# Convolution stage of a two-layer Fourier kernel: reciprocals and angle rounding in smaller pieces, second-half moments and v's statistics at later steps

## The chip, the cores and the metric

The kernel runs on one core of one Trainium2 chip. The metric is the device time of one execution in microseconds (us). Before the change it is 2817.53 us, the median of three runs that lie between 2812.63 and 2821.07. The profiled execution spans 2806.7 us, at a mean granted TensorE clock of 0.976 of full speed.

Engine names are those of the profile: PE is TensorE's matmul, PEld its weight load, DVE is VectorE, ACT is ScalarE, POOL is GpSimd, SP is SyncE, whose queue (SPq) issues nearly all transfers of this stage.

## The reference

The input x has shape 16 x 16 x 256 x 256 (images, channels, rows, columns), float32. Two layers follow each other:

```python
x = x + _L0_conv_ref(_gn(x), L0_conv_weight)      # a circular 3x3 convolution, written with FFTs
x = x + _L1_conv_ref(_gn(x), ty, tx, poles1, poles2, residues)   # a Laplace neural operator

def _gn(v, G=8, eps=1e-5):       # group norm: 8 groups of 2 channels, per image
    g = v.reshape(B_, G, C_ // G, H_, W_)
    m = jnp.mean(g, axis=(2, 3, 4), keepdims=True)
    s = jnp.var(g, axis=(2, 3, 4), keepdims=True)
    return ((g - m) / jnp.sqrt(s + eps)).reshape(v.shape)
```

Layer 1 needs tables made of the poles: reciprocals `1 / (omega - pole)` for all frequencies, and exponentials `exp(pole * t)`, whose imaginary part asks for sines of large angles, rounded to within pi first. These tables depend on the small weights alone, not on x.

## The kernel before

The kernel has four stages, one after the other: the convolution (about 29 to 642 us), the spectra (to about 1290 us), the mixing of channels (to about 1990 us), and the way back to the output. The change lies wholly in the first.

**The loop of the convolution stage.** `for g in range(24 * B + 3)` walks 387 steps, 24 for each of 16 images. Below, n is the step within an image, g modulo 24. At each step `conv(g)` (L225) issues 16 small matmuls (32 x 32 weights against 32 x 512 data, two records of line L239 each in the trace) that run side by side on four row groups and four column groups of the array. Every third step two PSUM tiles are full, and ACT evicts them as `vt` (L256), adds the bias and, by accumulators, their sums and squares. DVE then makes first moments of v from a quarter of the tiles (`bn_stats`, L258), and two steps later the mirrored sum and difference of lower and upper rows (`mirror`, L221 and L222, 128 x 1024 each). SP stores both to `vD` a step after that (L282).

**What else is put between the steps.** All engines execute their own instructions in the order in which the Python program emits them, so the loop's body is a schedule written by hand. At each step, in this order: `conv(g)`; one piece of `early`; loads of x; pieces of `x_stats` that are due; pieces of the two chains of tables.

- *Loads of x*: image b+2's first half at n = 3 and second half at n = 15 (L113, 2322 KB each, five buffers `xt`).
- *`x_stats(b)`* (L149) computes the group norm of image b, and with it the scaled weights `wc` and the bias, before step 24b. It yields pairs of a due time (steps before 24b) and a piece: 16 `moments` (`bn_stats`, L156), eight for each half of the image; `bn_aggr` (L164); a small matmul over the channels (`spread`, L168); `about_mean` (L176 to L178); a second `spread`; `root` (L184 on DVE, then a square root on ACT, L185); `conv_weights` (L144 to L201); a third `spread`; `biases` (L207, L208). The three matmuls stand in PE's order among those of the convolution, so PE stops at each until DVE has delivered its operand. They share one PSUM buffer, `ps_stat`. The bias column lies in the tile `xq`, of which there are two in turn.
- *Two chains of tables* of layer 1. One advances a piece every second step: `make_poles`, `make_hat` (twice two halves, with a reciprocal of 128 x 512, L420), `make_c` (eight rounds, with a reciprocal of 128 x 512, L566). The other advances a piece every fifth step: `make_exps` (twice eight rounds, with three `scalar_tensor_tensor` and two `tensor_scalar` for the rounding of the angles, L496 to L498), `make_coef`.
- *`early`*, a generator of `v_stats` (L291), turns the sums of the first 12 images of v into the scale and mean of layer 1's group norm. It has six pieces: many small DVE operations, a matmul (L312), more of them (L314 to L324), a matmul (L332), a square root, and a last refinement with two reciprocals of 128 x 192. Its two matmuls write `ps_stat` too. It advances when `g > 24 * (B - 4) + 8 and g % 3 == 0`, so at steps 9, 12, 15, 18, 21 and 24 after g = 288.

Of the kernel before, what the change touches and what calls it, by code (L numbers as in the profile page):

```python
# [16 lines left out]
B = 16  # L17
# [7 lines left out]
def conv_then_laplace_kernel(ctx: ExitStack, tc: tile.TileContext, a: dict, out: bass.AP):  # L25
# [15 lines left out]
    nc = tc.nc  # L41
# [83 lines left out]
    g128 = load1("g128", [P, P], tp)  # L125
# [23 lines left out]
    def x_stats(b):  # L149


        st = sp.tile([P, C, 6], FP, name="xst", tag="xst")

        def moments(j):
            r0 = 1 + 2 * (j % 8)
            nc.vector.bn_stats(st[:, j, :], halves[b][j // 8][:, r0 : r0 + 2, 1 : N + 1])  # L156

        for j in range(8):
            yield 38 - j, lambda: moments(j)
        for j in range(8, C):  # L160
            yield 33 - j // 2, lambda: moments(j)
        q = sp.tile([P, 12], FP, name="xq", tag="xq")
        mean, pvar, mu, d, e, var, sd, tmp, r, nb, bias = (q[:, j : j + 1] for j in range(11))
        yield 24, lambda: nc.vector.bn_aggr(q[:, 0:2], st)  # L164

        def spread(lhs, rhs):
            ps = pst.tile([P, 512], FP, name="ps_stat", tag="ps_stat")
            nc.tensor.matmul(ps[:, 0:1], lhsT=lhs, rhs=rhs, start=True, stop=True)  # L168
            return ps[:, 0:1]

        ps = []
        yield 18, lambda: ps.append(spread(g128, mean))

        def about_mean():

            nc.vector.tensor_copy(mu, ps[0])  # L176
            nc.vector.tensor_tensor(d, mean, mu, ALU.subtract)
            nc.vector.scalar_tensor_tensor(e, d, d, pvar, ALU.mult, ALU.add)  # L178

        yield 17, about_mean  # L180
        yield 14, lambda: ps.append(spread(g128, e))

        def root():
            nc.vector.tensor_scalar(var, ps[1], 1e-5, None, ALU.add)  # L184
            nc.scalar.activation(sd, var, AF.Sqrt)  # L185

        yield 12, root
        wc = sp.tile([P, 2, 3, 32], FP, name="wc", tag="wc")

        def conv_weights():  # L190
            newton(sd, var, tmp)
            nc.vector.reciprocal(r, sd)
            nc.vector.scalar_tensor_tensor(
                wc.rearrange("p h t m -> p (h t m)"),
                wband.rearrange("p h t m -> p (h t m)"),
                r,
                imask.rearrange("p h t m -> p (h t m)"),
                ALU.mult,
                ALU.add,
            )  # L200
            nc.vector.tensor_scalar(nb, mu, r, -1.0, ALU.mult, ALU.mult)  # L201

        yield 9, conv_weights
        yield 5, lambda: ps.append(spread(wsum.rearrange("p c m -> p (c m)"), nb))

        def biases():
            nc.vector.tensor_copy(bias, ps[2])  # L207
            nc.vector.tensor_scalar(shift[:, b : b + 1], mu, -1.0, None, ALU.mult)  # L208
            ready[b] = wc, bias

        yield 3, biases
# [171 lines left out]
    def make_hat(side):  # L383

        hatT = wp.tile([P, 6 * N], FP, name="hatT", tag="hatT")
        hatT = hatT[:, 0 : 2 * N].rearrange("p (j e t) -> p j e t", j=2, e=2)  # L390
        nc.sync.dma_start(out=hatT, in_=a[f"hatT{side}"])
        om = sw.tile([P, 3], FP, name="s_kcol", tag="s_kcol")
        nc.sync.dma_start(out=om[:, 0:1], in_=a["kcol"])
        om1, om2, scale = (om[:, j : j + 1] for j in range(3))
        to = ((tabE[:, 1:], tabO[:, :C]), (hB[:, 0], hB[:, 1]))[side]
        n = C * C * 2
        for half in range(2):
            tags = "s_re0", "s_re1", "s_pb", "s_im0", "s_im1", "s_den0", "s_den1"
            tiles = [
                sw.tile([P, 2 * n if t == "s_pb" else n], FP, name=t, tag=t)[:, 0:n] for t in tags  # L400
            ]
            pr, npi, m, sq, nb, g, b2 = tiles
            at = slice(half * n, half * n + n)
            for j in range(5):
                nc.sync.dma_start(out=tiles[j], in_=hD[j, side, at].partition_broadcast(P))
            yield
            yield
            if half == 0:
                omega(om1, om1, rd[:, side : side + 1])
                nc.vector.tensor_tensor(om2, om1, om1, ALU.mult)  # L410
                nc.vector.tensor_scalar(scale, cols[:, 17:18], -1.0, 1.0, ALU.mult, ALU.add)
                nc.vector.tensor_tensor(scale, scale, om1, ALU.add)
                nc.vector.tensor_scalar(hatT[:, 1], hatT[:, 1], scale, None, ALU.mult)
            yield
            nc.scalar.activation(g, sq, AF.Square, bias=om2)
            nc.scalar.activation(b2, nb, AF.Square)
            yield
            nc.gpsimd.tensor_tensor(g, g, b2, ALU.add)
            yield
            nc.vector.reciprocal(g, g)  # L420
            yield
            for z in (pr, npi, nb):
                nc.gpsimd.tensor_tensor(z, z, g, ALU.mult)
            yield
            nc.vector.scalar_tensor_tensor(sq, sq, om2, g, ALU.add, ALU.mult)
            yield
            nc.vector.scalar_tensor_tensor(pr, m, om2, pr, ALU.add, ALU.mult)
            nc.vector.scalar_tensor_tensor(npi, m, om2, npi, ALU.subtract, ALU.mult)
            for j, z in ((5, sq), (6, nb)):
                nc.sync.dma_start(out=z[0:1], in_=hD[j, side, at].unsqueeze(0))  # L430
            yield
            yield
            for eo in range(2):
                hv = to[eo].rearrange("p i (m r) -> p i m r", r=2)[:, 8 * half : 8 * half + 8]
                for ri, parts in enumerate(((pr, sq), (npi, nb))):
                    ps = psu.tile([P, 512], FP, name="ps_setup", tag="ps_setup")
                    for j, src in enumerate(parts):
                        nc.tensor.matmul(
                            ps, lhsT=hatT[:, j, eo], rhs=src, start=j == 0, stop=j == 1
                        )  # L440
                    yield
                    nc.scalar.copy(hv[:, :, :, ri], ps.rearrange("p (i m) -> p i m", i=8))
                    yield
# [24 lines left out]
    def make_exps(which):  # L468
# [10 lines left out]
        for q in range(8):  # L479
# [13 lines left out]
            c2 = float(np.float32(1.93500518798828125e-3))  # L493
            c3 = 2 * np.pi - c1 - c2
            for c in (c1, c2, c3):
                nc.vector.scalar_tensor_tensor(th, rn, -float(c), th, ALU.mult, ALU.add)  # L496
            nc.vector.tensor_scalar(th, th, phase, 3.1415925, ALU.add, ALU.min)
            nc.vector.tensor_scalar(th, th, -3.1415925, None, ALU.max)  # L498
            yield
# [14 lines left out]
    def make_c():  # L514
# [8 lines left out]
        z = space[:, 2 * N : 2 * N + 64].rearrange("p (j k) -> p j k", j=4)  # L523
# [30 lines left out]
        for k0 in range(0, C, 2):  # L554

            at = k0 // 2 % 2
            den = sw.tile([P, 2, N], FP, name="s_cden", tag=f"s_den{at}")
# [5 lines left out]
                nc.gpsimd.tensor_scalar(den[:, j], den[:, j], pr2[:, k : k + 1], None, ALU.add)  # L563
                nc.gpsimd.tensor_scalar(num[:, j], om, nm1, s0[:, k : k + 1], ALU.mult, ALU.add)
            yield
            nc.vector.reciprocal(den, den)  # L566
            w = sw.tile([P, 2, 4, 2, 4, 8], FP, name="s_w", tag=f"s_im{at}")
            for odd in range(2):
                for st in range(2):
# [10 lines left out]
                        ALU.mult,  # L580
                    )
            yield
            yield
            nc.gpsimd.tensor_tensor(num, num, den, ALU.mult)
            yield
# [2 lines left out]
            for i0 in range(0, 4, 2):  # L588
                c = c4[:, i0 : i0 + 2]
                ps = psu.tile([P, 2, N], FP, name="ps_setup", tag="ps_setup")  # L590
# [22 lines left out]
    def chain(*gens):  # L613
        for gen in gens:
            yield from gen
# [8 lines left out]
    for b in range(1, B):  # L624
        at_step.setdefault(max(0, 24 * b - 40), []).append((b, x_stats(b)))
    going = []
    tables = (
        (2, 0, chain(make_poles(), make_hat(0), make_hat(1), make_c())),
        (5, 1, chain(make_exps(0), make_exps(1), make_coef())),
    )  # L630
    early = v_stats(0, B - 4, lambda: pst.tile([P, 512], FP, name="ps_stat", tag="ps_stat"))
    for g in range(24 * B + 3):
        conv(g)
        if g > 24 * (B - 4) + 8 and g % 3 == 0:
            next(early, None)
        b, n = divmod(g, 24)
        if b + 2 < B and n == 3:
            halves[b + 2] = [load_x(b + 2, 0)]
        if b + 2 < B and n == 15:
            halves[b + 2].append(load_x(b + 2, 1))  # L640
        for b, gen in at_step.get(g, ()):
            going.append([b, gen, next(gen)])
        for it in list(going):
            while it[2] is not None and g >= 24 * it[0] - it[2][0]:
                it[2][1]()
                it[2] = next(it[1], None)
            if it[2] is None:
                going.remove(it)
        for every, first, gen in tables:
            if g % every == first:  # L650
                next(gen, None)
# [30 lines left out]
    m, n = cols[:, 16:17], cols[:, 17:18]  # L682
# [773 lines left out]
```

## Time and profile before

| | busy, us | share of the span |
|---|---|---|
| PE | 2616.8 | 93% |
| DVE | 1928.3 | 69% |
| ACT | 1522.8 | 54% |
| POOL | 1075.6 | 38% |

These shares cover the whole execution. The convolution stage is read by itself: the trace gives the busy time of every engine in any stretch, and the starts of the convolution's matmuls, 32 records to a step, tell when each step began. From these starts the 16 images took, in us: 35.4, 46.3, 38.3, 36.3, 50.6, 41.2, 34.2, 37.5, 34.5, 36.9, 36.7, 36.8, 50.4, 40.2, 28.9 and 28.3 (the last with the loop's end). The page's list of costliest groups gives for each line its busy time, the mean of one instruction, and how long the engine was idle just before it and for whom. The list of waits sums those idle times by waiting line and releaser. A window's timeline lists the instructions in order of time.

### The profile page before, as it was taken

Reading aid. Unit: us, or ns where it says so; the run is one execution under the profiler, and the core shown is the slowest. Engines: PE = TensorE matmul, PEld = TensorE weight load, DVE = VectorE, ACT = ScalarE, POOL = GpSimd, SP = SyncE. Lnnn points to the kernel's source line nnn. Section 1 sums busy time; section 2 is a strip of 40 time slices with the busy share of each in tenths; the row PEclk is TensorE's granted clock in tenths of the full one; section 3 lists DMA queues with packets and bytes.
Section 4 is the critical chain, followed back from the end, with each engine's and each line's share of the span. In section 5 each row is a group of like instructions: output and inputs, shape, how many; then the busy total and the mean of one; then the engine's idle time right before and its main releaser. Section 6 shows DMA issues by size and latency. Waiting matters only on the chain.

```text
span 2806.7 us, 93073 instructions
## 1 busy us (share of the span) xinstructions
PE 2616.8 (93%) x39600; PEld 1958.4 (70%) x39600; DVE 1928.3 (69%) x3562; ACT 1522.8 (54%) x3090; POOL 1075.6 (38%) x997
## 2 busy tenths in 40 slices
PE   5878988797999999996999999999989999999998
PEld 2434444355777777774888888888778888888887
DVE  6888998867888888885454444444346666666666
ACT  3767777664666666663455555555434444444443
POOL 1543466513333333334111111111165656565653
PEclk9999999898999999998999999999999999999999
DMA  7776887655665656654766666676688999989995
GB/s 270 255 248 247 286 285 267 230 185 166 229 229 208 213 203 240 227 193 162 200 189 194 190 192 192 194 195 193 198 274 284 289 284 288 283 286 286 288 284 179
DMA packets 479375, 652.82 MB, mean 233 GB/s; under 512 B 51352, under 2 KB 457880, under 8 KB 465008
## 3 DMA queue, kind: packets, MB, share of 16 engines
q1 hardware_dynamic: 477248, 637.56, 70.5%
q8 instruction: 312, 5.11, 0.7%
q0 software_dynamic: 1568, 5.11, 0.6%
q10 hardware_dynamic: 144, 4.19, 0.3%
q14 instruction: 103, 0.84, 0.1%
HBM read 367.22 MB, written 279.50 MB: 230 GB/s over the span
## 4 chain that ended last, share of the span: by engine, by line
PE 61%; DVE 14%; DMA 12%; POOL 4%; issue 4%; SPq 2%; ACT 1%; DVEq 0%; POOLq 0%; ACTq 0%
PE ps_mix L1028 16%; PE ps_s L962 9%; PE ps_y L720 8%; PE ps_y L728 8%; DMA yk<-yD 6%; PE ps_x L763 4%; PE ps_conv L239 4%; PE ps_p L1212 3%; DVE r L1245 3%; PE ps_f L1236 3%; PE ps_f L1237 3%; DMA out_y<-ol 3%; DVE xst L156 2%; DMA xt<-in_x 2%; SPq L1159 2%
## 5 line engine op out<-in xcount | busy, mean ns | idle before, releaser
L1028 PEld LDWEIGHTS ps_mix<-abd,sg 128*64 128x64 f32 x8192 | 449.1, 138 | 61.5 <-ACT sg L1085 48.9
L1028 PE MATMUL ps_mix<-abd,sg 128*64 128x128 f32 x8192 | 480.0, 276 | 9.5 <-ACT yt L1090 9.5
L239 PE MATMUL ps_conv<-xt,wc 32*32 32x512 f32 x12288 | 463.3, 618 | 27.2 <-issue 24.8
L1176 POOL TENSOR_TENSOR u<-yk 128x512 f32<-128x512 f32 (+1 forms) x268 | 346.0, 1322 | 317.7 <-PE ps_p L1212 210.3
L736 ACT ACTIVATE t<-ps_y,vmr 128x384 f32<-128x384 f32 x512 | 297.2, 581 | 166.7 <-PE ps_y L728 166.6
L239 PEld LDWEIGHTS ps_conv<-xt,wc 32*32 32x32 f32 x12288 | 231.4, 105 | 214.4 <-issue 139.4
L933 POOL TENSOR_TENSOR w<-v,mcol 128x2048 f32<-128x2048 f32 x33 | 119.3, 3616 | 575.3 <-DVE v L930 546.9
L1090 DVE COPY yt<-ps_mix 128x512 f32<-128x512 f32 x128 | 88.5, 691 | 360.7 <-PE ps_mix L1028 238.5
L720 PE MATMUL ps_y<-tabE,vq 128*128 128x256 f32 x1024 | 313.5, 388 | 15.0 <-DVE vq L709 13.4
L728 PE MATMUL ps_y<-tabO,vq 128*128 128x256 f32 x1024 | 306.1, 381 | 0.0
L1236 PE MATMUL ps_f<-pt,inv 128*128 128x256 f32 x1008 | 300.4, 380 | 0.0
L1090 ACT COPY yt<-ps_mix 128x512 f32<-128x512 f32 x384 | 220.5, 586 | 146.5 <-PE ps_mix L1028 88.4
L1237 PE MATMUL ps_f<-hs,ey 128*128 128x256 f32 x1008 | 299.8, 379 | 0.0
L1212 PEld LDWEIGHTS ps_p<-inv,u 128*128 128x128 f32 x2048 | 266.0, 193 | 45.0 <-issue 25.1
L1212 PE MATMUL ps_p<-inv,u 128*128 128x128 f32 x2048 | 279.4, 280 | 8.4 <-POOL u L1180 8.3
L962 PE MATMUL ps_s<-ct,w 64*32 64x256 f32 x8448 | 261.2, 382 | 24.4 <-POOL abd L977 24.1
L1240 DVE TENSOR_TENSOR r<-ps_f,q 128x256 f32<-128x256 f32 x256 | 106.9, 418 | 251.5 <-ACT q L1239 251.5
L1085 ACT COPY sg<-ps_s 128x512 f32<-128x512 f32 x248 | 159.7, 645 | 190.7 <-PE ps_s L962 190.6
L720 PEld LDWEIGHTS ps_y<-tabE,vq 128*128 128x128 f32 x1024 | 189.7, 191 | 91.5 <-ACT q L776 50.3
L256 ACT ACTIVATE vt<-ps_conv,xq 128x512 f32<-128x512 f32 x256 | 167.0, 680 | 155.9 <-PE ps_conv L239 140.7
L1239 ACT COPY q<-ps_f 128x256 f32<-128x256 f32 x256 | 95.4, 372 | 287.6 <-PE ps_f L1237 284.4
L1214 ACT COPY pt<-ps_p 128x512 f32<-128x512 f32 x256 | 150.1, 586 | 133.3 <-PE ps_p L1212 117.9
(238 smaller groups left out, 4170.4 us busy)
## 6 DMA issues: line engine op xcount, KB each, us to landing
xt<-in_x SPq DMA_DIRECT2D x32, 2322.0 KB, 10.8
abd<-aD SPq DMA_DIRECT2D x512, 128.0 KB, 2.9
yD<-yt SPq DMA_DIRECT2D x512, 128.0 KB, 2.6
vl<-vD SPq DMA_DIRECT2D x256, 256.0 KB, 4.1
out_y<-ol SPq DMA_DIRECT2D x128, 512.0 KB, 9.2
s<-vD SPq DMA_DIRECT2D x244, 256.0 KB, 6.7
aD<-spec SPq DMA_DIRECT2D x15, 4096.0 KB, 12.5
yk<-yD SPq DMA_DIRECT2D x60, 1024.0 KB, 8.5
```

The costliest lines, as they stand in the source:

```text
L239: nc.tensor.matmul(acc[r][32 * c : 32 * c + 32], lhsT=ready[b][0][rows, phase, tap], rhs=halves[b][u // 2][rows, q : q + 5 : 4, 2 - tap : ...
L256: nc.scalar.activation(vt[:, r % 2], acc[r], AF.Identity, bias=ready[b][1], **by_sums)
L720: nc.tensor.matmul(ps[:, 0:N], lhsT=vf[:, xo, 0, j], rhs=tabE[:, 0 : i + 2 : i + 1], start=True, stop=False, skip_group_check=True,)
L728: nc.tensor.matmul(ps[:, P : P + N], lhsT=vf[:, xo, 1, j], rhs=tabO[:, i : C + 1 : C - i], start=False, stop=True, skip_group_check=True,)
L736: nc.scalar.activation(t[:, xo, j].rearrange("p l n -> p (l n)"), ps[:, 0:384], AF.Copy, scale=vmr[:, 0, b0 + j, i : i + 1],)
L962: nc.tensor.matmul(ps[odd][32 * iq : 32 * iq + 32, ro], lhsT=w[rows, iq, kk, ro], rhs=ct[rows, iq, kk], start=True, stop=True,)
L1028: nc.tensor.matmul(ps[64 * t : 64 * t + 64, j], lhsT=sg[:, f : f + 2].rearrange("p f m -> p (f m)"), rhs=abd[jq][:, :, 2 * t + cc, 2 * jj ...
L1090: (nc.vector.tensor_copy if m == 3 else nc.scalar.copy)(o, src)
L1176: nc.gpsimd.tensor_tensor(u[:, :, j].rearrange("p b (c n) -> p c b n", c=8), in0, in1, o)
L1212: nc.tensor.matmul(ps[:, at], lhsT=u[:, n], rhs=tab, start=True, stop=True)
L1236: nc.tensor.matmul(ps[:, e], lhsT=tab, rhs=pt[:, e], start=True, stop=False)
L1237: nc.tensor.matmul(ps[:, e], lhsT=ey[:, e], rhs=hs, start=False, stop=True)
```

## The change

Long DVE operations of the tables are cut, with a step of the loop between the pieces; the two chains of tables get other phases; the second half's moments come three steps later and the pieces that follow come one or two steps later; `early` gets its own list of steps. What it is for: other work of DVE that PE waits for should not queue behind a long piece, moments should not stand at the head of DVE's queue before their half image has landed, and the matmuls of `early` should not come between a `spread` and the piece that reads it.

```diff
@@ x_stats
         for j in range(8, C):
-            yield 33 - j // 2, lambda: moments(j)
+            yield 30 - j // 2, lambda: moments(j)
...
-        yield 24, lambda: nc.vector.bn_aggr(q[:, 0:2], st)
+        yield 22, lambda: nc.vector.bn_aggr(q[:, 0:2], st)
...
-        yield 18, lambda: ps.append(spread(g128, mean))
+        yield 17, lambda: ps.append(spread(g128, mean))
...
-        yield 17, about_mean
+        yield 16, about_mean
         yield 14, lambda: ps.append(spread(g128, e))
@@ make_hat
-            nc.vector.reciprocal(g, g)
-            yield
+            for z in (g[:, 0 : n // 2], g[:, n // 2 :]):
+                nc.vector.reciprocal(z, z)
+                yield
...
             nc.vector.scalar_tensor_tensor(pr, m, om2, pr, ALU.add, ALU.mult)
+            yield
             nc.vector.scalar_tensor_tensor(npi, m, om2, npi, ALU.subtract, ALU.mult)
@@ make_exps
             for c in (c1, c2, c3):
                 nc.vector.scalar_tensor_tensor(th, rn, -float(c), th, ALU.mult, ALU.add)
+                if c == c2:
+                    yield
@@ make_c
-            nc.vector.reciprocal(den, den)
+            nc.vector.reciprocal(den[:, 0], den[:, 0])
...
             yield
+            nc.vector.reciprocal(den[:, 1], den[:, 1])
             yield
             nc.gpsimd.tensor_tensor(num, num, den, ALU.mult)
@@ the loop
-        (5, 1, chain(make_exps(0), make_exps(1), make_coef())),
+        (4, 1, chain(make_exps(0), make_exps(1), make_coef())),
...
-        if g > 24 * (B - 4) + 8 and g % 3 == 0:
+        if g - 24 * (B - 4) in (9, 14, 17, 38, 41, 44):
             next(early, None)
```

The chain of `make_exps` advances every fourth step instead of every fifth, and has five yields to a round instead of four, so a round takes 20 steps as before. A half of `make_hat` takes 20 yields instead of 18.

## Prediction

> **What bounds the kernel now.** I read the page's time slices first. The first nine of 40 slices (70 us each) are the convolution stage; PE is busy 0.5 to 0.9 there, DVE about 0.8 to 0.9. So the stage isn't bound by matmuls alone. I then asked for the busy time in stretches that begin with each image. Columns: stretch, its length, then busy us of PE, PEld, DVE, ACT, POOL (with instruction counts), granted clock, DMA share, GB/s. Images 1, 4, 8, 12, 13, 14 and 15:
>
> ```profile
> 64.90:111.20 46.30, 37.02 (x817) 17.97 (x794) 38.92 (x61) 27.16 (x62) 24.49 (x16) 0.93 0.73 238
> ...
> 185.80:236.40 50.60, 38.11 (x812) 17.61 (x784) 42.57 (x66) 27.01 (x61) 15.88 (x11) 0.90 0.61 213
> ...
> 349.30:383.80 34.50, 31.59 (x825) 16.55 (x800) 33.88 (x50) 29.42 (x68) 26.17 (x27) 0.95 0.82 283
> ...
> 494.20:544.60 50.40, 36.28 (x850) 16.16 (x823) 44.96 (x82) 29.07 (x67) 32.92 (x38) 0.83 0.59 207
> 544.60:584.80 40.20, 31.99 (x820) 15.88 (x806) 32.32 (x52) 28.51 (x69) 5.81 (x4) 0.92 0.73 245
> 584.80:613.70 28.90, 27.34 (x777) 15.84 (x780) 21.09 (x54) 20.04 (x52) 0.00 (x0) 1.00 0.49 168
> 613.70:642.00 28.30, 28.30 (x844) 20.51 (x812) 14.44 (x16) 22.95 (x59) 8.92 (x12) 1.00 0.69 227
> ```
>
> Without DVE's table work an image takes 28 to 29 us, PE's own pace. Image 8 takes 34.5 us, of which DVE is busy 33.9: there DVE is the bound and nothing is left to win but its work. Over images 1 to 13 (64.9 to 584.8 us, one stretch) DVE is busy 452.8 of 519.9 us. Its 67.1 us of idle time are all that a new order can win there, and most of them lie in images 1, 4, 5, 12 and 13.
>
> Next the waits, DVE's own in the stage (line, releaser: us in total, times, longest), then PE's:
>
> ```profile
> DVE xst L156 <- DMA xt<-in_x: 21.6, 6, 7.5
> DVE xq L164 <- ACT vt L256: 15.9, 5, 6.5
> DVE vsum L221 <- ACT vt L256: 12.0, 7, 3.3
> DVE s_cden L566 <- POOL s_cden L563: 3.6, 3, 2.1
> ```
> ```profile
> PE ps_stat L168 <- DVE xq L164: 39.7, 7, 25.1
> PE ps_stat L168 <- DVE xq L178: 12.4, 5, 6.7
> PE ps_stat L312 <- DVE xq L184: 8.8, 1, 8.8
> PE ps_stat L168 <- DVE vmr L343: 5.3, 1, 5.3
> ```
>
> The first of PE's rows has 25.1 us of the start in it. The last is the third `spread` of an image, held because `early` still reads `ps_stat` (L343). PE stops at the small matmuls until DVE gets to their operand; DVE stops at moments whose half image hasn't landed, and at `bn_aggr`, which overwrites the `xq` tile whose bias ACT still reads at the eviction of n = 2. Each stop of one makes the other late.
>
> **What the Trainium skill says.** "TensorE: Matmul & The Clock Gate", its table at the top, gives VectorE a strict first-in-first-out queue; the trace agrees: before 187.0 us DVE stands 7.5 us at a `bn_stats`, while the evictions for the `mirror` behind it end by 184.5. "VectorE: DVE Perf Modes", The TRN2 errata, says that an operation pays a fixed latency per instruction, so cutting costs something. The trace has a reciprocal of 512 columns at 3.34 us and of 192 at 1.34, so 6.25 ns a column and 0.14 us fixed. "Perfetto Trace Analysis", Identifying the Most-Contended Engine, takes occupancy as fair for VectorE; 87% here agrees.
>
> **The change part by part.**
>
> *Second half's moments, three steps later.* Their loads are issued at n = 15 and take 10.8 us (median). Of DVE's waits for x, those before second halves are 5.5 us (image 1), 7.5 (4), 4.4 (13) and 0.4 (12), 17.8 together. Now `biases` (0.2 us) and `mirror` (1.2 + 1.4) come first, about 2.8 us. Full use gives 2.5 x 3 + 0.4, about 8; at image 13 `mirror` itself isn't ready until 585.2, so 6 is the low end. I take -8, because table pieces come ahead as well. First halves (2.2 and 1.6 us) keep their waits.
>
> *`bn_aggr` two steps later.* It then stands behind the eviction that it waits for. That wait is 15.9 us, but where DVE has run ahead it would wait at the next `mirror` instead (12.0 us there already), so between 0 and -15; I take a quarter, -4. The slack from `bn_aggr` to the first `spread` shrinks from six steps to five, from `about_mean` to the second from three to two. Behind `about_mean` DVE has only a `bn_stats` and pieces ready anyway, and PE two steps (2 us) against 0.6 us of work for three small operations: nothing where DVE is the bound.
>
> *`early` at other steps.* Now the matmul of L312 is emitted before `root` at the same step, and must wait for it (8.8 us) because both use `ps_stat`; the later stop is 5.3 us. At steps 14 and 17 of an image the buffer is free. DVE works on through both: its idle time in images 12 and 13 is 5.4 + 7.9 = 13.3 us. The 12 us of DVE work of `early` stay, half of it moves to image 13, still full. Of the idle time 2.1 and 2.8 us follow directly from PE's stops (DVE then waits for evictions at L221 and L164); with the small ones I take -4, range -1 to -9.
>
> *Tables stretched.* 1 + 1 yields in each of four half hats is 8 yields, 16 steps; `make_c` ends at step 354 instead of 338, in image 14, where DVE idles 7.8 us. About one round's reciprocal leaves the bound part: -3.5.
>
> *Reciprocals in halves.* Twelve more instructions at 0.14 us: +1.7. A first half needs only the first half of `s_cden`, so half of the 3.6 us wait for POOL goes: -2. The halves and the split rounding (2 operations, then 3, 0.77 us each at most) shorten PE's stops, from 3.3 to 1.7 us a piece, but DVE works meanwhile; worth nothing by itself. The extra yield between `pr` and `npi` is alike.
>
> *Phases 2 and 4.* At odd and even steps the two chains no longer fall on one step (at 508 to 515 us they made one block of 7.3 us). Same DVE work, so nothing counted.
>
> Sum: -8 - 4 - 4 - 3.5 + 1.7 - 2 = -19.8 us. The stages behind don't change. 2817.5 - 19.8 = 2797.7, so 2798.
>
> **The rivals.**
>
> *The idle time forms anew.* DVE's wait for x becomes a wait at `mirror` or `vsum`, PE's stop at L164 is only moved; what remains is `make_c`'s tail and a little: about -4, so 2813. For it: DVE's idle time is as small as 0.6 to 4 us an image in images 6 to 11, and PE's mid-step stops ("issue", 24.8 us, PE waiting for nothing that is shown) are untouched. Against it: the five bad images have named causes that the change addresses.
>
> *Slower.* The tighter chain makes PE stop at the second `spread` in every image: +1 us for each of 15 images, +1.7 of instructions: 2834. The 12.4 us there now, with three steps of slack, speak for it; against it, PE isn't what lasts longest in images 1 to 13.
>
> *Much faster.* If one large stop feeds the next (image 4's late x, PE's 14.9 us step, image 5's 6.5 us wait), removing the first removes all; idle falls from 67 to 25 us: -42, 2776. Transfers speak against more: 0.8 of their share is busy in images 6 to 10 at about 280 GB/s.
>
> **How the numbers follow.** The forecast gets 0.53, much faster 0.15, no change 0.17, slower 0.15. Within 0.3% is 8.5 us. Faster 0.68, same 0.17, slower 0.15. The range goes from the much-faster case, 2774, to half way to the slower one, 2822: it leaves out about 0.1 on each side or less.
>
> **What would show it.** Right: images 4 and 12 drop by 5 us or more each; DVE's wait at L156 falls from 21.6 to some 13 us; PE's waits at L312 for L184 and at L168 for L343 vanish; the stage's last matmul ends near 622 us; DVE's busy time in the stage stays within 3 us. Wrong: a larger wait of PE at L168 for L178, larger waits of DVE at L221, or a first half's moments that wait longer because DVE arrives earlier.

## The result, and the profile after

The changed kernel takes 2801.27 us (median of six runs, 2795.73 to 2805.62); the kernel before, run beside it, 2816.26 us. The ratio is 0.9947, with a 95% interval of 0.9929 to 0.9965: about 15 us faster, where 19.8 were forecast. The gain lies in the convolution stage: its last matmul starts at 626.1 us instead of 641.7 in the two profiled executions.

The same stretches as before, one for each image, here of the changed kernel (stretch, length, busy us of PE, PEld, DVE, ACT, POOL, clock, DMA share, GB/s); images 1, 4, 6, 8, 12, 13, 14:

```profile
64.10:109.20 45.10, 35.95 (x816) 15.69 (x790) 36.88 (x62) 30.21 (x67) 21.33 (x17) 1.00 0.75 269
...
185.10:228.40 43.30, 34.28 (x805) 17.21 (x779) 36.90 (x60) 29.78 (x66) 16.98 (x13) 0.92 0.70 246
...
268.10:313.20 45.10, 38.55 (x808) 17.80 (x778) 32.58 (x55) 27.32 (x62) 19.69 (x15) 0.92 0.65 231
...
348.30:381.80 33.50, 31.26 (x833) 17.07 (x812) 32.98 (x55) 29.15 (x69) 25.96 (x26) 0.95 0.85 309
...
485.00:527.40 42.40, 33.98 (x834) 17.00 (x808) 38.64 (x72) 29.98 (x71) 29.86 (x29) 0.88 0.78 270
527.40:565.10 37.70, 33.43 (x837) 17.71 (x814) 36.75 (x58) 27.38 (x68) 22.21 (x28) 0.91 0.73 262
565.10:597.70 32.60, 29.06 (x806) 15.27 (x810) 25.78 (x60) 20.92 (x57) 1.27 (x1) 1.00 0.44 150
```

Images 4 and 12 lost 7.3 and 8.0 us, as forecast. But image 6 went from 34.2 to 45.1 us and image 14 from 28.9 to 32.6: something was given back. The list of waits shows where to look. DVE's own, and three rows of PE's (line, releaser: total us, times, longest):

```profile
DVE vsum L221 <- ACT vt L256: 20.0, 11, 2.9
DVE s_th L498 <- POOL s_rn L492: 15.0, 7, 4.1
DVE xq L176 <- PE ps_stat L168: 8.1, 3, 4.4
DVE xq L164 <- ACT vt L256: 7.3, 3, 4.0
```
```profile
PE ps_stat L168 <- DVE xq L164: 32.0, 6, 25.0
PE ps_stat L168 <- DVE xq L178: 23.2, 10, 6.6
PE ps_stat L168 <- DVE vs L314: 1.8, 1, 1.8
```

The wait for x, 21.6 us before, is gone altogether. PE's stops for `early` are down from 8.8 + 5.3 to 1.8. In their place stands a row that had 4.0 us before: the rounding of the angles (L498 now) waits 15.0 us for POOL, and PE's stops at the second `spread` (L178) rose from 12.4 to 23.2. The row of the rounding in the kernel before, and the stretch of images 1 to 13, before and after:

```profile
DVE s_th L496 <- POOL s_rn L490: 4.0, 2, 2.2
```
```profile
64.90:584.80 519.90, 437.69 (x10408) 212.99 (x10385) 452.77 (x713) 370.17 (x850) 259.21 (x239) 0.94 0.75 256
```
```profile
64.10:565.10 501.00, 431.80 (x10384) 213.70 (x10360) 436.33 (x719) 368.43 (x846) 255.30 (x239) 0.95 0.77 266
```

The stretch shrank from 519.9 to 501.0 us, yet DVE's idle time in it only from 67.1 to 64.7; DVE's busy time fell instead, from 452.8 to 436.3. The total is near the forecast, the composition is not. So each part was undone in the changed kernel, and two were made alone.

### The profile page after: what moved, and what is told of

It reads as the page before. It is cut to its first block, busy times and chain, and to the rows that moved or that the text cites. A ratio compares the mean times of both kernels' runs of the same rounds, so it can differ in the third digit from the quotient of the medians.

```text
span 2793.9 us, 93071 instructions
## 1 busy us (share of the span) xinstructions
PE 2610.7 (93%) x39600; PEld 1957.2 (70%) x39600; DVE 1927.0 (69%) x3574; ACT 1516.3 (54%) x3089; POOL 1076.8 (39%) x997
## 4 chain that ended last, share of the span: by engine, by line
PE 68%; DVE 10%; DMA 8%; POOL 5%; issue 4%; ACT 2%; SPq 2%; DVEq 0%; ACTq 0%; POOLq 0%
PE ps_mix L1033 16%; PE ps_s L967 9%; PE ps_y L725 8%; PE ps_y L733 8%; PE ps_p L1217 6%; PE ps_f L1241 5%; PE ps_f L1242 5%; PE ps_x L768 4%; PE ps_conv L239 4%; DMA yk<-yD 2%; DVE r L1250 2%; DMA out_y<-ol 2%; PE psd L753 1%; DVE xst L156 1%; PE ps_h L1201 1%
## 5 line engine op out<-in xcount | busy, mean ns | idle before, releaser
L725 PE MATMUL ps_y<-tabE,vq 128*128 128x256 f32 x1024 | 313.0, 387 | 14.0 <-DVE vq L714 12.4
L967 PEld LDWEIGHTS ps_s<-ct,w 64*32 64x32 f32 x8448 | 158.9, 106 | 91.6 <-POOL abd L982 25.1
## 6 DMA issues: line engine op xcount, KB each, us to landing
aD<-spec SPq DMA_DIRECT2D x15, 4096.0 KB, 12.4
```

The source lines that it names most:

```text
L725: nc.tensor.matmul(ps[:, 0:N], lhsT=vf[:, xo, 0, j], rhs=tabE[:, 0 : i + 2 : i + 1], start=True, stop=False, skip_group_check=True,)
L967: nc.tensor.matmul(ps[odd][32 * iq : 32 * iq + 32, ro], lhsT=w[rows, iq, kk, ro], rhs=ct[rows, iq, kk], start=True, stop=True,)
```

## Experiments: the parts

Ratios below are to the kernel before, run on the same chip, with 95% intervals. "Idle" is DVE's idle time over images 1 to 13 of the profiled run.

**The later moments undone** (all the rest as changed):

```diff
-            yield 30 - j // 2, lambda: moments(j)
+            yield 33 - j // 2, lambda: moments(j)
```

> The changed kernel, with the second half's moments back at their old steps (n = 19 to 22). Theory 1 (the later moments bring most of the gain, since DVE no longer stands at a half image that has not landed): 8 us or more of the 15 are lost, so about 2809 us, and DVE's waits for x at L156 return to 10 us or more. Theory 2 (the tables bring most: DVE work leaves images 1 to 13 and no longer falls on one step): within 3 us of the changed kernel, about 2801 us, and DVE's waits for x stay under 5 us.

2817.97 us, ratio 1.0017 (1.0009 to 1.0026). All of the gain is lost and a little more, and DVE's wait for x is back at 13.1 us. Everything else in the change, without this line, makes the kernel slightly slower.

**The later moments alone**, in the kernel before:

> The kernel before, with nothing but the second half's moments three steps later. Theory 1 as it stands now (undoing this edit in the changed kernel lost 18 us; the later moments bring the gain alone): ratio to the kernel before 0.993 to 0.996, about 2798 us, and DVE's waits for x at L156 under 3 us from 21.6. Rival (the gain needs the moved bn_aggr and about_mean with it): ratio 0.997 to 1.000, and DVE waits for ACT at bn_aggr 15 us or more as before.

2797.95 us, ratio 0.9936 (0.9917 to 0.9954): the whole gain, from one line. The stretch of images 1 to 13, with the columns as above:

```profile
62.40:568.10 505.70, 436.98 (x10412) 213.95 (x10390) 453.24 (x713) 371.11 (x852) 261.00 (x239) 0.96 0.76 266
```

DVE's busy time is what it was (453.2), its idle time 52.5 us against 67.1: here the gain has the form that the prediction gave it. No wait for x is left in DVE's list, which begins so:

```profile
DVE vsum L221 <- ACT vt L256: 25.1, 14, 2.7
DVE xq L164 <- ACT vt L256: 7.2, 2, 4.2
```

`bn_aggr` waits 7.2 us instead of 15.9: its due time is unchanged, but it follows the last moments, which now come at n = 1 instead of n = 22, so it is emitted at n = 1 and no longer at n = 0. The wait at `mirror` (L221) rose from 12.0 to 25.1 us, so part of the idle time did form anew.

**Is it the wait for x, or the order of DVE's work?** Later moments also let `biases` and `mirror`, and so stores and loads, come earlier. To tell these apart, the moments stay at their old steps in the kernel before, and those of the second half read the first half's tile, which landed long before. This kernel leaves out the statistics of the second half, so its normalisation isn't that of the reference:

```diff
-            nc.vector.bn_stats(st[:, j, :], halves[b][j // 8][:, r0 : r0 + 2, 1 : N + 1])
+            nc.vector.bn_stats(st[:, j, :], halves[b][0][:, r0 : r0 + 2, 1 : N + 1])
```

> The kernel before, with one difference: the second half's moments read the first half's tile, which landed long before (so the normalisation uses the moments of half of each image). Order, steps and work of all engines are as before; only the wait for the second half is gone. Theory W (the later moments help because DVE no longer stands at x that has not landed): ratio 0.992 to 0.996, like only_moments (0.9936). Theory O (they help because biases and mirror, and with these the stores and the next loads, come ahead of eight moments): ratio 0.998 to 1.001 although DVE's waits for x at second halves are gone.

2799.41 us, ratio 0.9953 (0.9936 to 0.9970), idle 54.5 us. Order and work are those of the kernel before, so taking away the wait for the half image is enough for a gain of about 13 us, without any move. That the later moments alone bring 18 isn't clear of noise, as the intervals overlap. The list of DVE's waits in this run has a lesson of its own:

```profile
DVE xq L164 <- ACT vt L256: 25.0, 5, 9.7
DVE vsum L221 <- ACT vt L256: 12.2, 9, 2.5
DVE xst L156 <- DMA xt<-in_x: 4.3, 2, 2.3
```

The row of `bn_aggr` is larger than before (25.0 against 15.9), and the kernel is faster all the same. The size of such a row alone doesn't say what it costs. The likely reading is that DVE, no longer held by x, arrives earlier and waits for the pace of PE and ACT there; no run isolates this.

**`bn_aggr`, the first `spread` and `about_mean` at their old due times:**

```diff
-        yield 22, lambda: nc.vector.bn_aggr(q[:, 0:2], st)
+        yield 24, lambda: nc.vector.bn_aggr(q[:, 0:2], st)
...
-        yield 17, lambda: ps.append(spread(g128, mean))
+        yield 18, lambda: ps.append(spread(g128, mean))
...
-        yield 16, about_mean
+        yield 17, about_mean
```

> The changed kernel, with bn_aggr, the first spread and about_mean back at due times 24, 18 and 17 (bn_aggr then comes right behind the last moments, at n = 1). Theory 1: about 4 us slower than the changed kernel, 2805 us, with DVE's wait at bn_aggr for ACT's eviction back at about 15 us from 7.3. Theory 2: no difference, 2801 us, since the wait only moves to the next mirror. Third theory (the tighter chain costs: PE's stops at the second spread for L178 rose from 12.4 to 23.2 us): 3 to 8 us faster, about 2796 us, with that row back near 12 us.

2800.78 us, ratio 0.9960 (0.9945 to 0.9974), against 0.9947 for the changed kernel: the intervals overlap, so a gain of 4 us isn't told apart from none. The time is that of the second theory, but DVE's waits fit neither of the first two: at `bn_aggr` 8.7 us instead of 7.3, far from 15, and at `mirror` 25.8 instead of 20.0, a rise where the second theory needs a fall. By its order in the program, `bn_aggr` stands at n = 1 here and at n = 2 in the changed kernel, since the last moments hold it; only one of the two steps is undone. The third theory falls: PE's row for L178 stays at 20.7 us without the tighter chain, so that chain isn't what raised it.

**`early` at its old steps:**

```diff
-        if g - 24 * (B - 4) in (9, 14, 17, 38, 41, 44):
+        if g > 24 * (B - 4) + 8 and g % 3 == 0:
```

> The changed kernel, with the statistics of v (early) back at steps 9, 12, 15, 18, 21 and 24 of image 12. As predicted: 4 us slower, 2805 us; image 12 returns from 42 to about 50 us and image 13 drops from 38 to about 34. Rival (half of early's DVE work only moved from image 12 to 13): within 2 us of the changed kernel, about 2801 us.

2802.56 us, ratio 0.9968 (0.9952 to 0.9983). That is 0.0021 worse than the changed kernel, some 6 us, with intervals that still overlap. PE's stops at L312 and for L343 come back at 1.3 and 3.7 us, well under the 8.8 and 5.3 of the kernel before. Images 12 and 13 take 45.1 and 40.4 us instead of 42.4 and 37.7, where about 50 and 34 were expected, and this can't decide: images 0 to 11, in which the two programs are the same, already take 7.0 us longer in this trace. Whether `early` gains anything, or its work was only moved, stays open.

**All edits of the tables undone** (whole reciprocals, whole rounding, phases 2 and 5):

```diff
-            for z in (g[:, 0 : n // 2], g[:, n // 2 :]):
-                nc.vector.reciprocal(z, z)
-                yield
+            nc.vector.reciprocal(g, g)
+            yield
...
-                if c == c2:
-                    yield
...
-            nc.vector.reciprocal(den[:, 0], den[:, 0])
+            nc.vector.reciprocal(den, den)
...
-        (4, 1, chain(make_exps(0), make_exps(1), make_coef())),
+        (5, 1, chain(make_exps(0), make_exps(1), make_coef())),
```

> The changed kernel, with all edits of the tables undone: whole reciprocals, whole rounding, phases 2 and 5. Theory 1: 2 to 4 us slower, about 2804 us. Theory 2: 8 us or more slower, about 2810 us, with about 4 us of DVE work back from image 14 in images 1 to 13. Third theory (the new waits of DVE at the rounding for POOL, 15.0 us, eat what the tables gain): 0 to 5 us faster, about 2798 us.

2791.01 us, ratio 0.9922 (0.9906 to 0.9938): about 7 us less than the changed kernel, with intervals that overlap a little (0.9929 to 0.9938). That the edits of the tables cost time is clear from the next run, whose interval lies above 1.

**The tables' edits alone**, in the kernel before:

> The kernel before, with nothing but the tables' edits (halves, split rounding, phases 2 and 4). If edits add up (undoing them in the changed kernel gained 0.25%): ratio 1.002 to 1.006, about 2825 us, with DVE's wait at the rounding for POOL at 12 us or more. Rival (the tables pay only without the later moments, since they spread work away from the late moments): ratio 0.995 to 0.999.

2820.50 us, ratio 1.0024 (1.0015 to 1.0032): slower by about as much. The stretches of images 1 to 13, the tables' edits alone first, then the change without them:

```profile
63.50:591.60 528.10, 438.59 (x10380) 215.10 (x10358) 442.17 (x722) 369.30 (x845) 257.14 (x239) 0.94 0.74 252
```
```profile
63.20:562.30 499.10, 439.84 (x10407) 212.95 (x10388) 451.99 (x711) 369.67 (x851) 259.85 (x239) 0.96 0.78 269
```

Alone, the edits take 10.6 us of DVE work out of these images (452.8 to 442.2), and add 18.8 us of idle time (67.1 to 85.9). The prediction had the first as a gain of 3.5 us and didn't have the second.

## Experiments: what in the tables costs

The rounding has to wait for three operations of POOL (L489 to L492) that are emitted one piece earlier in its chain. In the kernel before that is five steps, in the changed one four, and POOL's own queue may hold eight operations of `make_c` (L565 to L568) ahead of them. The changed kernel's timeline of POOL and DVE (start, us, engine, line, operation; idle time before in brackets):

```profile
459.03 1.77 POOL L567 TENSOR_SCALAR s_cden<-s_cden,s_space 128x256 f32<-128x256 f32 x1
...
462.78 1.82 POOL L487 TENSOR_SCALAR s_th<-s_t,s_pim 128x256 f32<-128x256 f32 x2
...
467.07 1.50 POOL L492 TENSOR_SCALAR s_rn<-s_rn 128x512 f32<-128x512 f32 x1
...
468.60 1.74 DVE L498 SCALAR_TENSOR_TENSOR s_th<-s_rn,s_th 128x512 f32<-128x512 f32 x1 [4.14 <-POOL s_rn L492]
```

`about_mean` ends at 464.5 and DVE then stands for 4.1 us at the rounding. Four kernels took this apart.

**The rounding whole and its chain at every fifth step again**, reciprocals in halves:

> The changed kernel, with the rounding of the angles whole again and its chain at every fifth step; reciprocals stay in halves. Theory P (the tables cost 8 us because the rounding comes four steps behind POOL's three operations instead of five, and DVE waits 15 us for POOL there): ratio 0.991 to 0.993, and DVE's wait at the rounding for POOL under 5 us. Theory H (the halves cost it: more pieces, tables that reach further into image 14): ratio 0.994 to 0.996 as for the changed kernel.

2793.59 us, ratio 0.9920 (0.9902 to 0.9938); DVE's wait at the rounding is 5.1 us. That is as good as without any edit of the tables (0.9922), though this interval too overlaps a little with that of the changed kernel.

**The reciprocals whole and the hats' yields as before**, the rounding split at every fourth step:

> The changed kernel, with whole reciprocals and the hats without the extra yields; the rounding stays split, at every fourth step. Theory P: ratio 0.994 to 0.996, no better than the changed kernel, with DVE's wait at the rounding for POOL still 10 us or more. Theory H: ratio 0.991 to 0.993.

2797.75 us, ratio 0.9942 (0.9926 to 0.9958): no better than the changed kernel, as theory P has it. Its number for the wait was wrong, though: the rounding waits only 4.6 us, and the whole reciprocal of `make_c` 8.1 us in its place:

```profile
DVE s_cden L568 <- POOL s_cden L565: 8.1, 6, 3.8
...
DVE s_th L496 <- POOL s_rn L490: 4.6, 2, 3.2
```

So the shorter period doesn't bring the 15.0 us by itself. The two chains share POOL's queue, and which of them waits depends on how their pieces fall together.

**A second step between POOL's operations and the rounding**, in the changed kernel, with the rounding whole so that a round keeps its 20 steps:

```diff
             nc.gpsimd.tensor_scalar(rn, rn, magic, None, ALU.subtract)
             yield
+            yield
...
-                if c == c2:
-                    yield
```

> The changed kernel, with the rounding whole again, but a second yield between POOL's three operations and the rounding (eight steps instead of four; a round still takes five yields at every fourth step). Theory P: the 15.0 us of DVE's waits for POOL there go, and the ratio is 0.990 to 0.993. Theory H: 0.994 to 0.996. If long pieces of DVE work matter by themselves (as the change's split rounding supposes), it is no better than the changed kernel although the wait for POOL is gone.

2787.28 us, ratio 0.9901 (0.9883 to 0.9919), from four runs. The wait at the rounding is 0.9 us, idle 53.8 us, and images 1 to 13 take 492.0 us:

```profile
DVE s_th L499 <- POOL s_rn L492: 0.9, 2, 0.7
```
```profile
63.40:555.40 492.00, 434.16 (x10381) 213.33 (x10357) 438.17 (x717) 367.80 (x844) 253.35 (x239) 0.95 0.78 272
```

This beats both the changed kernel and the one before: its interval lies below that of the changed kernel and below 1. From the change without its edits of the tables (0.9922, 0.9906 to 0.9938) it isn't told apart. It keeps the work that the tables' edits moved out of these images (438.2 us busy, against 452.8 before) and drops the wait that they had brought. Two things differ from the changed kernel here, the distance to POOL and the rounding in one piece; no run keeps the split rounding at the longer distance.

**The same with whole reciprocals:**

> The version with the second yield after POOL's operations (ratio 0.990), with whole reciprocals and the hats' old yields. If the halves are worth nothing, as predicted: ratio 0.989 to 0.992. If shorter pieces matter: 0.993 or more. If the halves' extra yields cost by a longer tail in image 14: 0.988 or less.

2796.16 us, ratio 0.9937 (0.9923 to 0.9951). So with this step the halves are worth about 10 us, where the prediction had them worth about nothing (+1.7 - 2); in the other two pairs (0.9947 with and 0.9942 without, 0.9920 and 0.9922) no gain shows. The list of DVE's waits in this run shows the row that the halves remove:

```profile
DVE s_cden L567 <- POOL s_cden L564: 8.8, 6, 3.9
```

With halves there is no such row (the first half reads one channel of the two, so it needs only half of POOL's work). The six kernels that differ in the tables alone, all with the other edits, make one picture when DVE's two waits for POOL are added up, at the rounding and at the reciprocals of `make_c`:

| tables | waits for POOL, us | ratio |
|---|---|---|
| second step before the whole rounding, halves | 0.9 | 0.9901 |
| as before the change | 3.8 | 0.9922 |
| whole rounding at every fifth step, halves | 5.1 | 0.9920 |
| second step before the whole rounding, whole reciprocals | 8.8 | 0.9937 |
| split rounding at every fourth step, whole reciprocals | 12.7 | 0.9942 |
| the changed kernel | 15.0 | 0.9947 |

From the first row to the last the wait grows by 14 us and the time, by the ratios, by about 13. The order was found afterwards, and the rows in the middle aren't clear of each other. It fits that these waits are what the tables cost, with either form of the rounding and of the reciprocals.

**`mirror` a step later**, in the same version with halves:

```diff
-                later.append((g + 2, lambda g=g, b=b, u=u, lo=acc["v", 0], hi=vt: mirror(g, b, u, lo, hi)))
+                later.append((g + 3, lambda g=g, b=b, u=u, lo=acc["v", 0], hi=vt: mirror(g, b, u, lo, hi)))
```

> The version with the second yield after POOL's operations, and mirror emitted three steps after the eviction instead of two. DVE's waits at mirror for ACT (24.9 us there, the largest row) should fall under 8 us. If these waits set the pace: ratio 0.985 to 0.988. If they only show DVE being ahead of PE, which then has to be waited for elsewhere: 0.989 to 0.992.

2794.82 us, ratio 0.9935 (0.9921 to 0.9949): slower than without it. The row at `mirror` did fall, from 24.9 to 11.1 us, but a wait for x came back that this version hadn't:

```profile
DVE xst L156 <- DMA xt<-in_x: 13.1, 5, 4.2
DVE vsum L221 <- ACT vt L256: 11.1, 9, 2.5
```

In SP's queue the loads of x stand behind the stores of `mirror`'s results. Argued from this order, a later `mirror` makes the loads late; the run shows only that the wait returns. Once more, cutting the largest row didn't make the kernel faster.

## Why the prediction was right, and where its steps were not

- **The bound** was read rightly: with one wait of DVE taken away and nothing else (the half image), the kernel got 13 us faster. One reading was off: the five images named hold 35.8 of the 67.1 us of idle time, and image 3, which isn't named, has the most (9.6). The upper end of the range is also a little under half way to the slower case (2817.5 to 2834); neither bears on the result.
- **Second half's moments, -8:** mechanism right, size too small. Alone they bring 0.64%, some 18 us, more than the whole change. The term counted what `biases` and `mirror` cover of each wait (2.8 us). In fact the whole row of 21.6 us went to nothing, first halves too (why these, stays open), and `bn_aggr`'s wait fell by 8.7, while `mirror`'s grew by 13.1, as the first rival had it; DVE's idle time fell by 14.6 in sum. The third rival, one stop feeding the next, isn't borne out: idle time fell to 52.5 us and not to 25, and with the wait for x alone removed `bn_aggr`'s wait grew.
- **`bn_aggr` two steps later, -4:** not told apart from nothing (0.0013, overlapping). Nearly all of the fall of its wait, 15.9 to 7.3, comes with the later moments alone (7.2), which move it by a step.
- **`early`, -4:** about 6 us by the ratios, not clear of nothing; PE's waits at L312 for L184 and at L168 for L343 vanished as forecast.
- **Tables stretched, -3.5; halves, +1.7 - 2; split rounding and phases, 0:** sum -3.8, measured about +7. This is the step that failed.
  - *The halves' own cost* was about right: 24 of 1.72 us are 41.2 us, against 40.1 for twelve whole ones, so 1.1 instead of 1.7. "VectorE: DVE Perf Modes" in the Trainium skill, The TRN2 errata, has a fixed latency per instruction, and these 0.1 us for each pair agree.
  - *Phases 2 and 4*, "same DVE work, so nothing counted", left out the wait for POOL: a piece in every chain has a distance in steps to the piece that feeds it, and the new period cut it from five to four. DVE's waits for POOL in both chains went from 7.6 us to 15.0: the 3.6 at the reciprocals went, more than forecast, and 11.0 came at the rounding, with the new period and the halves together. The trace before showed the row, 4.0 us in two waits, and I didn't ask what the change does to it. The tables also brought the extra of PE's row for L178: it is 34.3 us with the tables' edits alone and 12.6 in the change without them. That makes the sign of being wrong, a larger row for L178, come true, with another cause than the tighter chain; the larger waits at L221, a second such sign, came too.
  - *Tables stretched* was mis-sized. It counted on image 14 to take the work into DVE's idle time there; the tables' edits alone take 10.6 us of DVE work out of images 1 to 13 and not 3.5, but in the changed kernel image 14, with 4.7 us more of DVE work, is 3.7 us longer.
- **DVE's busy time within 3 us:** wrong. Over all sixteen images it fell by 9.6 us (518.6 to 509.0). Four lines of DVE operations with two inputs (L222, the rounding, L193, L221) are 6.7 us shorter in sum; the rest stays open.

A term that was too small and one with the wrong sign nearly cancel: about 18 us of gain from the moments, perhaps 4 to 10 from the two smaller moves, less 7 for the tables. These don't add up exactly to 15, since most ratios are uncertain by about 0.0017, 5 us. That the forecast of the direction held has its reason in the moments; that its size came out so near is in part luck.

## What to carry to other kernels

In a schedule written by hand, a piece's place is fixed by two distances: to the work that feeds it and to the work that waits for it. When a period or a number of pieces changes, count the first one anew for every engine in between, POOL and the transfers too. Judge a wait by removing its cause in a run, not by its size in the list: here one row grew from 15.9 to 25.0 us in a kernel that became faster, and another shrank from 24.9 to 11.1 in one that became slower, while removing the waits for x, 21.6 us at the head of DVE's queue, brought 13 to 18.

## What the runs showed of the hardware

A DVE `tensor_tensor` of 128 x 1024 (L222) takes 1.22 us on average where POOL has nothing running at the time (26 instructions of the kernel before) and 1.60 us where POOL runs for more than half of it (36). "GPSIMD Engine Reference" in the Trainium skill, 1. Specifications, says that POOL's SBUF interfaces are shared with VectorE and that DVE instructions with two SBUF inputs contend with it; this agrees. The same comparison for L221, of the same shape and also with two inputs, gives only 1.21 and 1.30 us, so the size is no constant. The busy time of DVE isn't either: it depends on what POOL does at the time, which may be part of the 9.6 us above, though no run isolated it.
